# A two-layer graph network on one core: the order of work in layer 0's rounds, and where the first maxima of the attention are searched

## The chip, the core and the metric

The kernel runs on one core of a Trainium2 chip. A core has TensorE (PE, matrix products), VectorE (DVE), ScalarE (ACT), GpSimd (POOL) and SyncE (SP), which here issues every DMA. The metric is the device time in microseconds (us) of one execution; lower is better.

## What is computed

There are N = 3327 nodes with 128 features, and a dense 0/1 adjacency matrix with ones on its diagonal. Two layers follow each other, each with a residual sum and a layer norm:

```python
# layer 0: attention by cosine over the neighbours
norm2 = norm(x, axis=1)
cos   = beta * (x @ x.T) / (norm2 @ norm2.T + 1e-7)
P     = softmax(cos + (1 - adj) * -1e9, axis=1)
x     = layernorm(x + P @ x)
# layer 1: 128 heads of width 8, all over the whole graph
q, k, v = (x @ W.T).reshape(128, n, 8)  for W in (Wq, Wk, Wv)
a   = softmax(einsum('dnh,dmh->dnm', q, k) * 128**-0.5 + adj + adj, axis=2)
out = einsum('dnm,dmh->dnh', a, v).reshape(n, 1024) @ Wo.T
x   = layernorm(x + out)
```

## The kernel before

All is in float32; q and k of layer 1 are split into a high and a low part. The nodes are padded to T = 26 tiles of 128. The program has four stages.

**Layer 0** runs in rounds. In round t four tiles of rows are in hand at once, at different steps, and a list written out by hand (the loop over k from 0 to 7) says in which order each engine takes them up. PE, ACT, DVE and POOL each work through their own list strictly in that order. The steps, with the lines of the profile:

- `load` (L120): a tile's 128 rows of the adjacency, 1.66 MB, into one of three buffers `raw`; SP issues it.
- `adj_chunk` 0 to 6 (L166, L215): PE turns four 128x128 blocks of `raw` into a PSUM bank `tp`, ACT copies them into `aT`; with the seventh, SP writes the turned tile to memory for layer 1. There are two banks `tp`, shared with the turns of the weights.
- `mask` (L221): one POOL pass over `raw`, in place; it waits until PE has turned the last chunk.
- `inverse_log`, `inverse_exp` (L228, L231): two long ACT passes that give 1/(product of norms) as `y`. `inverse_product`, `inverse_newton` (L236, L242): two long DVE passes that refine `y`; the first makes `n` from `norm_k` and `y`, the second `y` from `n` and `y`.
- `scores` 0 to 3 (L190, L250, L253): PE multiplies a quarter of the columns, DVE combines it with `y` and then adds the mask and keeps a running minimum.
- `weights` (L269): two ACT passes, the exponential. `turn_weights` 0 to 6 (L166, then a copy to `pt`): PE turns four blocks of the weights, and DVE (even chunks, L156) or ACT (odd chunks, L154) copies them. `weigh0` (L288): PE multiplies the copied chunk with the features. There are two buffers `pt`.
- `norm_begin`, `norm_root`, `norm_end` (L295 to L322): the layer norm, in small steps on DVE, ACT and DVE. `project_turn`, `project` 0 to 5 (L330 to L347): the rows of q, k and v, by PE through one PSUM bank, ACT, and a write by SP.

**Splitting q and k** (L453 to L491): for each of 8 groups of 16 heads, a strided read of k, of q and of v (`nat`), a POOL pass that reorders it (L458), and for k and q seven turns on PE, the rounded high part by ACT (L469), the rest by DVE (L470), a POOL copy of the last column (L473), and two writes of 1.66 MB. Here the order is found by the scheduler, not by hand.

**Attention**: 288 units, each three tiles of queries by four heads, with 26 steps of 128 keys. A softmax needs the greatest score of a row first: the maxima are searched `T + AHEAD` = 33 steps ahead of the main loop, each step a pair (PE L616, DVE L631 or L642) and a single (L616, L652 or L656). So before the main loop starts, 33 steps run alone, after the loads of the first two units (L563 to L575) and beside the loads of the first adjacency block (L540, 26 of 96 KB). Then 26 ACT passes make `eT` from them (L547), and the first exponentials of the main loop (L840) stand behind these on ACT.

**The end** turns and projects the rows and does the last layer norm.

Of the kernel before, what the change touches and what calls it, by code (L numbers as in the profile page):

```python
# [10 lines left out]
F32 = mybir.dt.float32  # L11
F32R = mybir.dt.float32r
BF16 = mybir.dt.bfloat16
# [3 lines left out]
PSUM = bass.MemoryType.PSUM  # L17
# [29 lines left out]
def gnn_two_layers(  # L47
# [104 lines left out]
    def copy(i: int, dst: bass.AP, src: bass.AP):  # L152
        if i % 2:
            nc.scalar.copy(dst, src)  # L154
        else:
            nc.vector.tensor_copy(dst, src)  # L156
# [18 lines left out]
    with ExitStack() as l0:  # L175
# [23 lines left out]
        def load(t: int):  # L199
            u = tiles[t]  # L200
            u.raw = load_adj(adj_raw, t)
            u.xr = ptp.tile([P, D], F32, name="xr", bufs=5)
            if t < T - 1:
                nc.sync.dma_start(u.xr, node_rows(x, t, D))
            else:
                nc.gpsimd.memset(u.xr, 0.0)
                nc.sync.dma_start(u.xr[: P - 1], node_rows(x, t, D, P - 1))
# [66 lines left out]
        def turn_weights(t: int, c: int):  # L274
            u = tiles[t]
            if c == 0:
                u.pts = {}
            tp, a, b = turn(ps_tp, lambda k: u.s[:, k * P : (k + 1) * P], c)
            u.pts[c] = ptp.tile([P, 4, P], F32, name="pt")[:, : b - a, :], a, b
            copy(c, u.pts[c][0], tp)  # L280

        def weigh0(t: int, c: int):
            u = tiles[t]
# [22 lines left out]
        def norm_root(t: int):  # L306

            u = tiles[t]
            u.r = small.tile([P, 1], F32, name="r0")
            nc.scalar.activation(u.r, u.var, AF.Ln)  # L310
            nc.scalar.activation(u.r, u.r, AF.Exp, scale=-0.5)
# [37 lines left out]
        with tc.manual_schedule(  # L349
# [53 lines left out]
                nc.scalar.activation(piece(norm_k, j), score_piece(ones, sqT, j), AF.Sqrt)  # L403
            nc.scalar.preload_act_table_set("natural_log_exp_and_others")

            for t in range(-1, T + 2):

                def there(n: int):
                    return 0 <= n < T

                for k in range(8):
                    if k == 0 and there(t + 2) and t > 0:
                        load(t + 2)
                    if k == 0 and there(t - 2):
                        norm_begin(t - 2)
                    if k == 0 and there(t - 1):
                        weights(t - 1, 0)
                        weights(t - 1, 1)
                    if k == 1 and there(t - 2):
                        norm_root(t - 2)  # L420
                    if there(t) and k in (0, 2, 4, 6):
                        scores(t, k // 2)
                    if k == 2 and there(t - 2):
                        norm_end(t - 2)
                    if k < NCH and there(t + 1):
                        adj_chunk(t + 1, k)
                    if k == 1 and there(t + 1):
                        inverse_log(t + 1)
                    if k == 2 and there(t + 1):
                        inverse_exp(t + 1)  # L430
                    if k > 0 and there(t - 1):
                        turn_weights(t - 1, k - 1)
                        if k > 1:
                            weigh0(t - 1, k - 2)
                    if k == 3 and there(t - 2):
                        project_turn(t - 2)
                    if there(t - 2):
                        for i in {4: (0,), 5: (1, 2), 6: (3,), 7: (4, 5)}.get(k, ()):
                            project(t - 2, i)
                    if k == 6 and there(t + 1):  # L440
                        mask(t + 1)
                    if k == 7 and there(t + 1):
                        inverse_product(t + 1)
                        inverse_newton(t + 1)
                if there(t - 1):
                    weigh0(t - 1, NCH - 1)


    with ExitStack() as pr:
        work = pr.enter_context(tc.tile_pool(name="pr_work", bufs=2))  # L450
        ps_tp = pr.enter_context(tc.tile_pool(name="pr_tp", bufs=4, space=PSUM))

        for g in range(NG):  # L453
            for src, dst in ((k_s, kp_s), (q_s, qp_s)):
                nat = work.tile([P, HG, T * H], F32, name="nat")
                nc.sync.dma_start(nat, heads(src)[g])
                by_t = work.tile([P, T, P], F32, name="by_t")
                nc.gpsimd.tensor_copy(  # L458
                    by_t.rearrange("p t (g h) -> p g t h", h=H),
                    nat.rearrange("p g (t h) -> p g t h", h=H),  # L460
                )

                high = work.tile([P, NP], F32R, name="high")
                low = work.tile([P, NP], F32R, name="low")
                for c in range(NCH):
                    tp, a, b = turn(ps_tp, lambda t: by_t[:, t], c)
                    cols = slice(a * P, b * P)
                    tp = tp.rearrange("p t k -> p (t k)")
                    nc.scalar.copy(high[:, cols], tp)  # L469
                    nc.vector.tensor_sub(low[:, cols], tp, high[:, cols].bitcast(F32))  # L470

                for i, part in enumerate((high, low)):
                    nc.gpsimd.tensor_copy(  # L473
                        part[:, NP - 1 : NP], part[:, NP - 1 - P : NP - P].bitcast(F32)
                    )
                    nc.sync.dma_start(
                        dst[g * HG : (g + 1) * HG, :, i].rearrange("d f n -> (d f) n"),
                        part.bitcast(F32),
                    )
            nat = work.tile([P, HG, T * H], F32, name="nat")  # L480
            nc.sync.dma_start(nat, heads(v_s)[g])
            vals = work.tile([P, HG, T, H + 1], F32, name="vals")
            nc.gpsimd.memset(vals[:, :, :, H : H + 1], 1.0)
            nc.gpsimd.tensor_copy(
                vals[:, :, :, :H], nat.rearrange("p g (t h) -> p g t h", h=H)
            )
            nc.vector.tensor_scalar_mul(vals[:, :, T - 1], vals[:, :, T - 1], real)
            nc.sync.dma_start(
                vt_s[4 * g : 4 * g + 4].rearrange("a p h t f -> p a (h t f)"),
                vals.rearrange("p (a h) t f -> p a (h t f)", a=4),  # L490
            )  # L491

# [3 lines left out]


    with ExitStack() as at:  # L500
        fix = at.enter_context(tc.tile_pool(name="at_fix", bufs=1))
        keys = at.enter_context(tc.tile_pool(name="at_k", bufs=3))
        pp = at.enter_context(tc.tile_pool(name="at_p", bufs=4))
        sm = at.enter_context(tc.tile_pool(name="at_sm", bufs=2))
        ps_a = at.enter_context(tc.tile_pool(name="at_a", bufs=2, space=PSUM))
        ps_b = at.enter_context(tc.tile_pool(name="at_b", bufs=1, space=PSUM))
        ps_m = at.enter_context(tc.tile_pool(name="at_m", bufs=1, space=PSUM))
        ps_o = at.enter_context(tc.tile_pool(name="at_o", bufs=1, space=PSUM))

        QB = QT * P  # L510
        AHEAD, LAG = 7, 2
        acc = ps_o.tile([P, 512], F32, name="acc")
        nc.vector.memset(acc, 0.0)
        one = fix.tile([P, P], BF16, name="one")
        nc.vector.tensor_copy(one, ones)
        unit = fix.tile([P, P], BF16, name="unit")
        nc.vector.tensor_copy(unit, ident)

        nine = fix.tile([P, 4, H + 1], F32, name="nine")
        nc.vector.tensor_copy(  # L520
            nine, ident.rearrange("p (h x) -> p h x", h=4)[:, :, : H + 1]
        )

        parts = []
        for i in range(2):
            three = fix.tile([P, QT, 4, 32], BF16, name=f"parts{i}")
            nc.vector.memset(three, 0.0)
            parts.append(three)
        aT = fix.tile([P, T, QB], BF16, name="aT1")
        eT = fix.tile([P, T, QB], F32, name="eT1")  # L530

        units = [(b, g) for b in range(NB) for g in range(G4)]
        NU = len(units)
# [246 lines left out]
        with tc.manual_schedule(  # L780
# [4 lines left out]
                mybir.EngineType.Pool,  # L785
            }
        ):
            us = {0: load_unit(0), 1: load_unit(1)}
            steps = {}

            def max_step(k):
# [5 lines left out]
                    steps[i] = max_steps(2 * i, 2 * i + 1)  # L797
                return steps[i][j]

            def new_a():  # L800
                return [ps_a.tile([P, 512], F32, name="ea") for _ in range(2)]

            for j in range(T):
                load_adj_tile(0, j)
            for k in range(T + AHEAD):
                pair, single = max_step(k)
                max_pair(*pair)
                max_single(*single)
                if k == T:
                    shift_parts(us[0])  # L810
            e = ps_b.tile([P, 2, 512], F32, name="eb")
            for q in range(QT):
                shift_turn(us[0], q, e[:, 0, q * P : (q + 1) * P], True)
# [155 lines left out]
```

## Time and profile before

| | |
|---|---|
| time, median of 3 runs | 16088.82 us (16087.31 to 16089.61) |
| the profiled execution | 16094.0 us, of which its span 16092.2 us |
| layer 0, up to the last row write | to 955.7 us of the span |
| one round of layer 0 (combine of score piece 0 to the next) | 34.15 us |
| splitting q and k | 955.9 to 1253.4 us |
| first maxima alone | 1262.3 to 1331.5 us |
| first exponential of the main loop | 1343.2 us |
| main loop to its end | to 15975 us |

Times of instructions are counted from the first instruction of the span. In an answer by windows the columns are the stretch, then for PE, its weight loads, DVE, ACT and POOL the busy microseconds with the number of instructions, then the granted TensorE clock (1.00 is full speed), the share of the DMA engines' time that was used, and GB/s. A line of the timeline has the start, the length, the engine, the code line, the operation, output and input, and in brackets how long the engine stood idle and who ended that. Matmuls overlap, so the time that one takes from its engine is the distance to the next start.

### The profile page before, as it was taken

Reading aid. Unit: us, or ns where it says so; the run is one execution under the profiler, and the core shown is the slowest. Engines: PE = TensorE matmul, PEld = TensorE weight load, DVE = VectorE, ACT = ScalarE, POOL = GpSimd, SP = SyncE. Lnnn points to the kernel's source line nnn. Section 1 sums busy time; section 2 is a strip of 40 time slices with the busy share of each in tenths; the row PEclk is TensorE's granted clock in tenths of the full one; section 3 lists DMA queues with packets and bytes.
Section 4 is the critical chain, followed back from the end, with each engine's and each line's share of the span. In section 5 each row is a group of like instructions: output and inputs, shape, how many; then the busy total and the mean of one; then the engine's idle time right before and its main releaser. Section 6 shows DMA issues by size and latency. Waiting matters only on the chain.

```text
span 16092.2 us, 507025 instructions
## 1 busy us (share of the span) xinstructions
PE 15517.9 (96%) x217532; PEld 6935.5 (43%) x217532; DVE 13906.8 (86%) x16159; ACT 12637.3 (79%) x24904; POOL 13664.8 (85%) x9062
## 2 busy tenths in 40 slices
PE   6748999999999999999999999999999999999999
PEld 5533444444444444444444444444444444444555
DVE  6637999999999999999999999999999999998775
ACT  5525888888888888888888888888888888888776
POOL 1016999999999999999999999999999999998886
PEclk9978999999999999999999999999999999999999
DMA  3372111111111111111111111111111111111112
GB/s 128 126 269 94 47 50 50 51 50 50 48 53 50 50 44 57 50 47 48 57 50 45 50 52 51 48 50 50 51 50 50 47 54 50 50 45 60 61 61 75
DMA packets 483008, 995.72 MB, mean 62 GB/s; under 512 B 280274, under 2 KB 377424, under 8 KB 436208
## 3 DMA queue, kind: packets, MB, share of 16 engines
q1 hardware_dynamic: 480752, 963.28, 17.6%
q8 instruction: 1704, 27.92, 0.7%
q14 instruction: 552, 4.52, 0.1%
HBM read 813.16 MB, written 149.94 MB: 60 GB/s over the span
## 4 chain that ended last, share of the span: by engine, by line
PE 92%; DVE 4%; ACT 2%; DMA 1%; issue 1%; POOL 0%; SPq 0%; DVEq 0%; POOLq 0%; ACTq 0%
PE acc L725 28%; PE ea L695 20%; PE m L616 15%; PE eb L708 12%; PE ea L708 9%; PE ea L714 2%; PE eb L714 2%; DVE mx L631 1%; PE ea L681 1%; PE tp L166 1%; PE ea L743 1%; PE acc L288 1%; DVE y L242 1%; DVE n L236 1%; PE pq L342 1%
## 5 line engine op out<-in xcount | busy, mean ns | idle before, releaser
L841 POOL TENSOR_TENSOR pb<-pb,eT 128x768 f32<-128x768 f32 (+1 forms) x7488 | 13181.4, 1765 | 1103.4 <-ACT pb L840 858.6
L631 DVE TENSOR_REDUCE mx<-m 128x2 f32<-128x1024 f32 x6784 | 8274.2, 1220 | 516.8 <-PE eb L714 249.7
L840 ACT ACTIVATE pb<-eb 128x768 f32<-128x768 f32 (+1 forms) x7488 | 5896.9, 788 | 2507.8 <-PE eb L714 1772.7
L616 PE MATMUL m<-kx,qx 32*128 32x512 f32 (+1 forms) x23296 | 6781.8, 471 | 70.8 <-DVE mx L631 38.2
L870 ACT ACTIVATE pa<-ea 128x384 f32<-128x384 f32 (+1 forms) x14976 | 6339.7, 478 | 59.0 <-PE ea L695 45.2
L725 PE MATMUL acc<-pa,vt 128*9 128x384 f32 (+1 forms) x29952 | 5901.7, 474 | 0.0
L725 PE MATMUL acc<-pb,vt 128*9 128x384 f32 (+1 forms) x29952 | 5900.0, 474 | 0.1
L652 DVE TENSOR_REDUCE mx<-m 128x1 f32<-128x512 f32 x6400 | 4380.8, 685 | 691.1 <-PE m L616 317.9
L708 PEld LDWEIGHTS <-one 3*128 3x128 bf16 x29952 | 1507.8, 91 | 5564.2 <-issue 4665.8
L695 PE MATMUL ea<-aT,two 128*32 128x384 bf16 (+1 forms) x59904 | 3714.5, 325 | 0.0
L714 PE MATMUL ea<-qx,kx 32*128 32x384 f32 (+1 forms) x14976 | 3447.5, 437 | 0.0
L714 PE MATMUL eb<-qx,kx 32*128 32x384 f32 (+1 forms) x14976 | 3435.3, 451 | 0.0
L708 PE MATMUL ea<-cx,one 3*128 3x384 bf16 (+1 forms) x14976 | 3293.8, 322 | 2.9 <-ACT pa L870 0.2
L616 PEld LDWEIGHTS m<-kx,qx 32*128 32x128 f32 x23296 | 2815.0, 182 | 443.8 <-DVE mx L631 96.0
L708 PE MATMUL eb<-cx,one 3*128 3x384 bf16 (+1 forms) x14976 | 2461.6, 326 | 9.5 <-ACT pb L840 8.9
L725 PEld LDWEIGHTS acc<-pa,vt 128*9 128x9 f32 x29952 | 1413.2, 91 | 786.5 <-issue 0.7
L695 PEld LDWEIGHTS <-two 128*32 128x32 bf16 x59904 | 944.8, 94 | 1418.4 <-issue 1278.4
L714 PEld LDWEIGHTS eb<-qx,kx 32*128 32x128 f32 x14976 | 1460.7, 189 | 0.0
L714 PEld LDWEIGHTS ea<-qx,kx 32*128 32x128 f32 x14976 | 1431.8, 182 | 8.2 <-issue 4.1
L725 PEld LDWEIGHTS acc<-pb,vt 128*9 128x9 f32 x29952 | 1409.3, 91 | 0.6 <-POOL pb L841 0.6
L656 DVE TENSOR_REDUCE mx<-m 128x2 f32<-128x512 f32 x1088 | 748.3, 688 | 96.7 <-PE eb L714 44.1
L221 POOL TENSOR_SCALAR raw<-raw 128x3328 f32<-128x3328 f32 x26 | 78.6, 3022 | 738.7 <-PE tp L166 727.9
(124 smaller groups left out, 4976.6 us busy)
## 6 DMA issues: line engine op xcount, KB each, us to landing
kx<-kp_s SPq DMA_DIRECT2D x576, 832.0 KB, 4.8
vt<-vt_s SPq DMA_DIRECT2D x288, 468.0 KB, 4.9
qx<-qp_s SPq DMA_DIRECT2D x1024, 48.0 KB, 5.1
raw<-in_adj_dram SPq DMA_DIRECT2D x25, 1663.5 KB, 7.7
aT_s<-aT SPq DMA_DIRECT2D x26, 832.0 KB, 3.4
aT<-aT_s SPq DMA_DIRECT2D x208, 96.0 KB, 2.1
vt_s<-vals SPq DMA_DIRECT2D x8, 1872.0 KB
q_s<-row SPq DMA_DIRECT2D x26, 512.0 KB, 2.6
```

Of the source, the lines that this page charges most:

```text
L166: nc.tensor.transpose(tp[:, i, :], block(4 * c + i), ident)
L616: nc.tensor.matmul(dst, u.qx[rows(a), q * P : (q + 1) * P], u.kx[rows(a), k0:k1], start=True, stop=True,)
L631: nc.vector.tensor_reduce(u.mx[:, h, qs[0], c], m, axis=AX.X, op=ALU.max)
L652: nc.vector.tensor_reduce(u.mx[:, a, qs[0], c : c + 1], m, axis=AX.X, op=ALU.max)
L656: nc.vector.tensor_reduce(u.mx[:, a, qs[0] : qs[1] + 1, c], m.rearrange("p (q k) -> p q k", q=2), axis=AX.X, op=ALU.max,)
L695: nc.tensor.matmul(e[r, : u.nq], two[:, r], aT[:, j, : u.nq], start=False, stop=True, tile_position=(0, 32 * c), skip_group_check=True,)
L708: nc.tensor.matmul(e[:, : u.nq], one[r], u.cx[r, : u.nq], start=True, stop=False, skip_group_check=True)
L714: nc.tensor.matmul(e[:, : u.nq], u.kx[rows(a), j * P : (j + 1) * P], u.qx[rows(a), : u.nq], start=False, stop=stop, skip_group_check=True,)
L725: nc.tensor.matmul(acc[32 * h : 32 * h + H + 1, : u.nq], u.vt[:, h, j], pts[h // 2][:, h % 2, : u.nq], start=(j == 0), stop=(j == T - 1), ...
L840: nc.scalar.activation(pt_b[:, :, : u.nq], e_b[:, :, : u.nq], AF.Exp)
L841: nc.gpsimd.tensor_tensor(pt_b[:, :, : u.nq], pt_b[:, :, : u.nq], eT[:, j, : u.nq].unsqueeze(1).to_broadcast([P, 2, u.nq]), ALU.mult,)
L870: nc.scalar.activation(pt_a[:, h, : u.nq], e[:, : u.nq], AF.Exp)
```

## The change

In layer 0, ACT's long passes of a round come first: the exponentials of tile t-1, the root of tile t-2's norm, and the two passes that make `y` of tile t+1. Score pieces 0 and 1 are done together at the start, then 2 and 3. The adjacency is turned and masked two tiles ahead instead of one, in the second half of the round, and loaded three tiles ahead; there is one round more, at the start. All copies of turned weights go to DVE. The two refining passes come at k = 6, ahead of the last turned chunk, and the mask at k = 7.

The stage that splits q and k is now written out by hand inside the attention's schedule. Units 0 and 1 are loaded after the first group, and three steps of the first maxima follow each of the k and q splits from group 2 on. The last column is copied by DVE instead of POOL, and `vals` has one buffer instead of two. The pools for `aT1`, `eT1` and the main loop are opened only after that stage, so the loads of the first adjacency block come after it.

```diff
@@ turn_weights
-            copy(c, u.pts[c][0], tp)
+            nc.vector.tensor_copy(u.pts[c][0], tp)
@@ rounds of layer 0
-            for t in range(-1, T + 2):
+            for t in range(-2, T + 2):
...
                 for k in range(8):
-                    if k == 0 and there(t + 2) and t > 0:
-                        load(t + 2)
                     if k == 0 and there(t - 2):
                         norm_begin(t - 2)
                     if k == 0 and there(t - 1):
                         weights(t - 1, 0)
                         weights(t - 1, 1)
+                    if k == 0 and there(t - 2):
+                        norm_root(t - 2)
+                    if there(t):
+                        for i in {0: (0, 1), 2: (2,), 4: (3,)}.get(k, ()):
+                            scores(t, i)
+                    if k == 0 and there(t + 1):
+                        inverse_log(t + 1)
+                        inverse_exp(t + 1)
                     if k == 1 and there(t - 2):
-                        norm_root(t - 2)
-                    if there(t) and k in (0, 2, 4, 6):
-                        scores(t, k // 2)
-                    if k == 2 and there(t - 2):
                         norm_end(t - 2)
-                    if k < NCH and there(t + 1):
-                        adj_chunk(t + 1, k)
-                    if k == 1 and there(t + 1):
-                        inverse_log(t + 1)
-                    if k == 2 and there(t + 1):
-                        inverse_exp(t + 1)
                     if k > 0 and there(t - 1):
                         turn_weights(t - 1, k - 1)
                         if k > 1:
                             weigh0(t - 1, k - 2)
                     if k == 3 and there(t - 2):
                         project_turn(t - 2)
+                    if there(t + 2):
+                        for i in {3: (0, 1), 4: (2,), 5: (3, 4), 6: (5,), 7: (6,)}.get(k, ()):
+                            adj_chunk(t + 2, i)
+                    if k == 5 and there(t + 3) and t >= 0:
+                        load(t + 3)
                     if there(t - 2):
                         for i in {4: (0,), 5: (1, 2), 6: (3,), 7: (4, 5)}.get(k, ()):
                             project(t - 2, i)
                     if k == 6 and there(t + 1):
-                        mask(t + 1)
-                    if k == 7 and there(t + 1):
                         inverse_product(t + 1)
                         inverse_newton(t + 1)
+                    if k == 7 and there(t + 2):
+                        mask(t + 2)
                 if there(t - 1):
                     weigh0(t - 1, NCH - 1)
@@ splitting q and k, now within the attention's hand-written schedule
-            us = {0: load_unit(0), 1: load_unit(1)}
+            us = {}
...
-            for j in range(T):
-                load_adj_tile(0, j)
-            for k in range(T + AHEAD):
+            def first_max(k):
                 pair, single = max_step(k)
                 max_pair(*pair)
                 max_single(*single)
                 if k == T:
                     shift_parts(us[0])
...
+                def prepare(g, src, dst):
...
+                    for i, part in enumerate((high, low)):
+                        nc.vector.tensor_copy(
+                            part[:, NP - 1 : NP], part[:, NP - 1 - P : NP - P].bitcast(F32)
+                        )
...
+                k = 0
+                for g in range(NG):
+                    for src, dst in ((k_s, kp_s), (q_s, qp_s)):
+                        prepare(g, src, dst)
+                        for _ in range(3 if g > 1 else 0):
+                            if k < T + AHEAD:
+                                first_max(k)
+                                k += 1
+                    prepare_values(g)
+                    if g == 0:
+                        us[0], us[1] = load_unit(0), load_unit(1)
+                while k < T + AHEAD:
+                    first_max(k)
+                    k += 1
+
+            fix = at.enter_context(tc.tile_pool(name="at_fix", bufs=1))
...
+            aT = fix.tile([P, T, QB], BF16, name="aT1")
+            eT = fix.tile([P, T, QB], F32, name="eT1")
+            for j in range(T):
+                load_adj_tile(0, j)
```

## The prediction

> **What bounds the kernel now.** I read the busy time by stage first, here layer 0 from its first combine, the split of q and k, the first maxima, and the main loop.
>
> ```profile
> 63.00:956.00 893.00, 676.70 (x3408) 513.25 (x3408) 564.36 (x753) 463.61 (x638) 77.87 (x51) 0.93 0.32 117
> 956.00:1253.00 297.00, 81.23 (x416) 73.59 (x416) 70.32 (x120) 58.94 (x112) 81.39 (x63) 0.60 1.03 375
> 1253.00:1333.00 80.00, 46.02 (x126) 20.42 (x126) 61.14 (x72) 0.93 (x3) 0.94 (x4) 0.50 0.41 122
> 1333.00:15975.00 14642.00, 14610.17 (x212849) 6238.69 (x212848) 13153.07 (x15068) 12075.19 (x24100) 13485.58 (x8923) 1.00 0.15 51
> ```
>
> The main loop is PE's (14610 of 14642) and its list is not changed: I take 0 for it. The split is the DMA engines' (share 1.03, no compute engine over 82 of 297). The maxima are DVE's (61 of 80). Layer 0 belongs to nobody: PE 676 of 893, DVE 564. So I read the chain of waits there; one round looks like this:
>
> ```profile
> 301.16 2.99 DVE s L253
> 304.49 3.60 DVE n L236
> 308.12 3.62 DVE y L242
> 314.14 2.97 ACT y L228
> 317.58 2.88 ACT y L231
> ```
>
> DVE's refining passes, then ACT's two passes with PE's copies behind them, 34.15 us a round. The minimum at 301.16 takes 2.99 where its sisters take 1.08: POOL's mask runs from 300.31 for 2.97. The start of the program shows what that pair does to the refining passes (timelines of DVE, then POOL):
>
> ```profile
> 52.91 3.69 DVE L236 SCALAR_TENSOR_TENSOR n<-norm_k,norm_c,y 128x3328 f32<-128x3328 f32 x1 [14.82 <-ACT y L231]
> 56.63 6.26 DVE L242 SCALAR_TENSOR_TENSOR y<-n,y 128x3328 f32<-128x3328 f32 x1
> ```
> ```profile
> 55.12 4.30 POOL L221 TENSOR_SCALAR raw<-raw 128x3328 f32<-128x3328 f32 x1 [14.31 <-PE tp L166]
> ```
>
> The mask is released during the first pass, waits for its end, and then runs before the second pass: 1.3 + 2.97 = 4.30, and the second pass takes 6.26 instead of 3.62. Last, PE's clock, in stretches as long as the clock's own steps (3.41 us):
>
> ```profile
> 317.50:320.92 3.42, 0.78 (x5) 0.53 (x4) 1.47 (x7) 3.42 (x4) 0.00 (x0) 1.00 0.06 19
> 320.92:324.33 3.41, 3.34 (x14) 3.17 (x15) 0.69 (x1) 0.77 (x3) 0.00 (x0) 0.50 0.00 0
> 1037.70:1041.10 3.40, 1.63 (x10) 1.04 (x10) 3.01 (x6) 1.45 (x3) 0.00 (x0) 1.00 1.03 410
> 1167.40:1170.80 3.40, 1.57 (x13) 1.21 (x11) 3.24 (x7) 2.20 (x5) 1.84 (x2) 1.00 1.11 347
> ```
>
> A stretch in which PE is busy 0.78 of 3.41 is followed by one at half clock, in every round. The same befell 1.63 at 1037.7, but not 1.57 at 1167.4, nor 1.74 at 95.6. The edge lies at some 1.6.
>
> **A round, walked through.** PE's prices are distances between starts:
>
> ```profile
> 326.37 1.06 PE L288 MATMUL acc<-xn,pt 128*128 128x128 f32 x8
> 327.26 1.02 PE L342 MATMUL pq<-wq,x1T 128*128 128x512 f32 x2
> 328.12 0.62 PE L166 MATMUL tp<-ident,raw 128*128 128x128 f32 x4
> 328.57 0.60 PE L166 MATMUL tp<-ident,s 128*128 128x128 f32 x4
> 329.01 1.06 PE L288 MATMUL acc<-xn,pt 128*128 128x128 f32 x8
> ```
>
> A weighing costs 0.89, a projection 0.86, a group of four turns 0.44; a score piece 1.4 (1.56 until DVE may read). On DVE a score piece takes 2.12, the norm's end 1.1, a copy 0.65. Zero is DVE's first combine. Scores 0 and 1 to 4.2, norm end to 5.3, copy 0 done at 6.0; score piece 2 to 8.0, copy 1 done at 8.7. Weighing 1 waits for that. From 8.7 PE has work in hand: weighings 1 to 3 (2.7), the turn of x1 (0.2), chunks 0 to 4 (2.2), scores 3 (1.4), turns 3 and 4 (0.9), projections 0 to 2 (2.6) and once the wait for the one bank (0.9, as at 331.62): 10.9, so turn 5 starts at 19.6. Its copy lets DVE begin the first refining pass at 20.9, to 24.6.
>
> Now the mask: it needs the last chunk, and PE gets there 0.44 + 0.89 + 0.44 + 0.86 + 0.22 + 0.89 + 0.38 = 4.1 after turn 5 starts, at 23.7: 0.9 before the first pass ends. That is the case of 55.12, so the second pass ends 6.3 later, at 30.9, not 3.6 later, at 28.3. Queued behind it on DVE stands the copy of chunk 6 (0.41), for which PE's weighing 6 waits, and behind that in PE's list scores 0 of the next round: 30.9 + 0.4 + 0.5 + 1.6 = 33.4 for the next combine. Before, at full clock, the round is 34.15 less what the half-clock stretch costs: 320.99 to 325.48 is 4.49 for work worth 0.44 + 0.89 + 0.2 + 1.4 = 2.93, thus 32.6. ACT's saving (the three copies, 1.75, and the wait of 2.63 behind its long passes) is spent: DVE takes the copies (+2.0), and what is late next is DVE's second pass.
>
> The clock: PE ends its last projection near 26.9 and waits over 4 us for weighing 6. A stretch of 3.41 with nearly nothing in it follows, so weighing 6 and scores 0 and 1 run at half clock: +1.9 on the way to the combine, +0.4 for piece 1: 35.7. A second place is the wait for copies 0 and 1: the 3.41 us before weighing 1 hold weighing 0 and a group of turns, 1.5 busy with their ends. That is below 1.63 and 1.57, so I take the half clock for the next stretch too; it costs 1.6 as before: **37.3**. Layer 0: 26 x (37.3 - 34.15) = **+82**. If the second stretch keeps its clock: 26 x 1.55 = +40.
>
> The Trainium skill (TensorE: Matmul & The Clock Gate, HAM oscillation) asks only that PE have no gap over some 3.4 us. In this trace the longest gap of a round, 2.63, already loses the clock, so the measurement decides; by the page alone the round would be 35.7.
>
> The rest of the rounds, edits with one answer: the load of tile t+3 goes out when score piece 3 frees its buffer, near 15, and is needed near 10 of the next round, over 25 us later against 7.7 to land: 0, and if SP held it so long, 26 times what is late. On SP it moves behind x1's write and ahead of the rows of q: 0.3 us of issue. The extra first round does work that is dropped later: 0.
>
> **The split and the maxima.** The 33 steps cost 2.12 each (1263.18, 1265.30), 70 us. In the new place they are 3 steps or 6.4 us of DVE per split, beside 37 us of DMA per group, in which DVE is busy 9: hidden; without that cover they cost up to 70. Against that:
> - Units 0 and 1 are now read while the DMA engines are full: 4.65 MB at 375 GB/s, 12. On SP these reads stand behind the first group's value write and ahead of the second group's key writes, and wait until the first group has landed (up to 17.1, as the value write issued at 1025.57); the engines are moving those writes meanwhile, so 0, with 10 as the upper end.
> - The first adjacency block waits until the split's buffers are free, that is for its last write:
>
> ```profile
> 1238.10 15.24 DMA vt_s<-vals
> 1257.15 5.21 DMA vt<-vt_s
> ```
> ```profile
> 1263.49 15.98 SPq L540 DMA_DIRECT2D aT<-aT_s  x26
> ```
>
> So 1253.4 + 12 = 1265.4; 26 issues 16.0; landing 2.1; the last exponential 0.5 (the others, 0.42 each, keep up with issues of 0.61): the main loop's first exponential at 1284 instead of 1343.2. Before, these loads lay under the maxima. Gain **-59**, with ends -45 (the 10 above and slower issues) and -65.
> - The copies of the last column on DVE: the rival below. One buffer of `vals`: a write is long landed when the next group's values come, 37 us later: 0.
>
> Sum on the profiled execution: 16094.0 + 82 - 59 = 16117. The median lies 5.2 below that execution: **16112**.
>
> **Rivals.**
> 1. *The clock falls once a round.* 1.57 busy kept it at 1167.4. Then 40 - 59 = -19: 16070. Chance 0.24.
> 2. *The mask comes too late to step between the passes.* If PE's list is 0.9 us later there, POOL takes its turn after the second pass and hits nothing. The round is 33.4 - 2.6 = 30.8 at full clock, with one or two half-clock stretches 32.4 to 34.1: -45 to 0, with the split -104 to -59, middle 16007. Against it: 4.1 us of list without a wait on another engine. Chance 0.12.
> 3. *Slower: the last-column copies, now from SBUF to SBUF on DVE, wait for POOL's reordering pass* (2.96 each), as the minimum waits for the mask. No row shows such a copy beside a POOL pass; bounds 0 and 16 x 2.96 = 47. It decides only where the write behind it comes after the DMA engines have run dry, that is where DMA's share falls below 1; today over 10 us of transfers wait in line mostly. I take 0. With 47: 16159. Chance 0.07.
>
> In the Trainium skill, SBUF — State Buffer (Who interferes with whom) lets a plain copy block that way, which speaks for rival 3 as a mechanism; no run here shows it for these copies.
>
> **How the numbers follow.** My forecast has 0.55, the others 0.24, 0.12 and 0.07, with 0.02 for what I do not see. The forecast's own spread is 15 us each way (14 between the ends of the split, a tenth of a microsecond or two per round): 16097 to 16128. About 0.2% (32 us, to 16121) is what a measurement of this kernel can tell from no change; a third of the forecast lies above it. Slower: 0.2 + 0.07 + 0.01 = 0.28. Faster (below 16057): 0.12 + a tenth of rival 1 and a little = 0.15. Same: 0.57. The range takes in rival 1 and the upper half of rival 2, and the spread upward with a third clock stretch: 16035 to 16145.
>
> **What would show it.** Right: rounds of 36 to 37.5 us; L242 at 6.2 with L221 starting during L236; two or three half-clock stretches a round; the maxima inside the split; first exponential of the main loop 50 to 60 us sooner after the split's start. Wrong: L242 at 3.6 in the rounds; rounds below 34; DMA's share in the split below 0.95, or a main loop that is not 14642 long.

## The result, and the profile after

The changed kernel takes 16068.7 us (median of 20 runs, 16065.2 to 16072.1), the kernel before 16086.8 us (20 runs, 16084.5 to 16089.6): a ratio of 0.9989, 95% interval 0.9982 to 0.9996. It is 18 us or 0.11% faster, less than the 0.2% that the prediction gives as what one measurement of this kernel can tell from no change. I had forecast 16112, 23 us above the old median. The sign was wrong, and by the parts below the error lies almost wholly in one term: the price of the half clock.

The busy time by stage after (layer 0 from its first combine, the split with the maxima in it, the loads of the first adjacency block, the main loop):

```profile
63.00:1007.50 944.50, 702.51 (x3401) 501.44 (x3400) 627.82 (x833) 432.08 (x556) 93.32 (x49) 0.87 0.29 111
1007.50:1316.00 308.50, 114.85 (x523) 89.70 (x523) 134.15 (x220) 58.77 (x112) 78.43 (x36) 0.61 1.01 376
1316.00:1333.50 17.50, 2.80 (x31) 1.65 (x32) 2.28 (x5) 12.30 (x28) 0.00 (x0) 0.50 0.78 186
1333.50:15950.00 14616.50, 14594.03 (x212806) 6251.14 (x212805) 13145.69 (x15066) 12061.30 (x24073) 13488.60 (x8922) 1.00 0.16 51
```

Layer 0 is longer (944.5 instead of 893), and its clock is granted at 0.87 instead of 0.93. The split is 11.5 longer and still full of DMA (share 1.01); DVE's busy time in it went from 70 to 134, the maxima that no longer stand by themselves. From its first to its last wide exponential the main loop takes 14617 instead of 14631, 14 less, which I had put at 0. (Its window before, 14642 long, begins 10 us ahead of the first exponential.)

The chain of waits in one round after:

```profile
501.64 6.26 DVE y L242
508.31 1.20 PE acc L288 x4
509.51 2.70 PE sc L190 x4
512.24 1.09 DVE s L250
```

The second refining pass, weighing 6, scores 0, the next combine: the way that the prediction walked. And POOL's mask in the next round (timeline of POOL, then of DVE):

```profile
537.00 3.51 POOL L221 TENSOR_SCALAR raw<-raw 128x3328 f32<-128x3328 f32 x1 [9.27 <-PE tp L166]
```
```profile
537.72 6.26 DVE L242 SCALAR_TENSOR_TENSOR y<-n,y 128x3328 f32<-128x3328 f32 x1
```

The mask is released 0.7 before the first pass ends (0.9 forecast), waits for that end, and the second pass waits for the mask: 6.26, in every full round. But the rounds come in pairs of 36.17 and 35.51, a mean of 35.84, and not the 37.3 of the forecast. In each round the clock falls to a half for two steps at weighing 6 and scores 0 (6.83 us); in every other round it falls once more, for one step, after the wait for copy 0. PE's clock over such a pair, in windows on the clock's own steps, with the weighing 0 that ends the wait (timeline of PE):

```profile
515.38:518.80 3.42, 1.11 (x9) 0.87 (x8) 3.24 (x10) 1.70 (x1) 0.00 (x0) 1.00 0.06 19
518.80:522.21 3.41, 3.17 (x15) 2.77 (x15) 2.72 (x5) 0.00 (x0) 0.00 (x0) 0.50 0.00 0
552.93:556.35 3.42, 1.59 (x12) 1.36 (x12) 3.28 (x7) 0.23 (x1) 0.00 (x0) 1.00 0.06 19
556.35:559.76 3.41, 2.57 (x19) 2.52 (x20) 1.38 (x4) 1.06 (x3) 0.00 (x0) 1.00 0.00 0
```
```profile
518.29 1.63 PE L288 MATMUL acc<-xn,pt 128*128 128x128 f32 x8 [2.31 <-DVE pt L280]
554.47 1.16 PE L288 MATMUL acc<-xn,pt 128*128 128x128 f32 x8 [1.68 <-DVE pt L280]
```

In one round the wait is 2.31 long and lies whole in one step, which is left with 1.11 of work; the next step runs at half clock. In the other round scores 0 and 1 ran at half clock for longer (5.02 instead of 4.29), so PE comes later to the same wait. It is 1.68 long, its step holds 1.59 of work, and the clock stays.

Behind layer 0, from the chain of waits:

```profile
1301.58 14.38 DMA vt_s<-vals
1329.66 2.96 DMA aT<-aT_s
```

The split's last write lands, 26 issues of 0.53 each follow (0.61 before), and the main loop's first exponential comes at 1333.5: 325.9 after the split's start, where it was 387.3.

### The profile page after: what moved, and what is told of

The parts are those of the page before. It is cut to its first block, busy times and chain, and to the rows that moved or that the text cites. A ratio compares the mean times of both kernels' runs of the same rounds, so it can differ in the third digit from the quotient of the medians.

```text
span 16067.9 us, 507030 instructions
## 1 busy us (share of the span) xinstructions
PE 15521.0 (97%) x217532; PEld 6936.2 (43%) x217532; DVE 13964.9 (87%) x16269; ACT 12606.0 (78%) x24826; POOL 13681.2 (85%) x9030
## 4 chain that ended last, share of the span: by engine, by line
PE 92%; DVE 5%; DMA 1%; ACT 0%; issue 0%; POOL 0%; SPq 0%; DVEq 0%; POOLq 0%; ACTq 0%
PE acc L663 28%; PE ea L633 20%; PE m L554 15%; PE eb L646 12%; PE ea L646 9%; PE eb L652 2%; PE ea L652 2%; DVE mx L569 1%; PE ea L619 1%; DVE y L242 1%; PE tp L166 1%; PE acc L288 1%; PE sc L190 1%; PE ea L681 1%; DVE mx L590 1%; DVE n L236 1%
## 5 line engine op out<-in xcount | busy, mean ns | idle before, releaser
L652 PE MATMUL eb<-qx,kx 32*128 32x384 f32 (+1 forms) x14976 | 3473.2, 454 | 0.0
```

The lines of the kernel that those rows point to most:

```text
L652: nc.tensor.matmul(e[:, : u.nq], u.kx[rows(a), j * P : (j + 1) * P], u.qx[rows(a), : u.nq], start=False, stop=stop, skip_group_check=True,)
```

## The experiments

Kernels that ran together share their runs of the kernel before: its median was 16086.2 beside the first four, 16092.1 beside the next four and 16092.0 beside the last. So each result is given as the difference to that as well. The changed kernel itself stands at -18.1, and "below the changed kernel" is counted from there. The theory at the start: the round goes through both refining passes, made long by the mask, and then through weighing 6 and scores 0, with a price for each half-clock stretch on top. Its rivals: the mask has nothing to do with it; the passes alone hold the round; the price of the clock is something else.

**e1 and e2, each half of the change alone.** e1 has the new layer 0 before the old split, e2 the old layer 0 before the new split.

```diff
 e1, layer 0 alone: the first part of the change
-            copy(c, u.pts[c][0], tp)
+            nc.vector.tensor_copy(u.pts[c][0], tp)
-            for t in range(-1, T + 2):
+            for t in range(-2, T + 2):
...
 e2, behind layer 0 alone: the second part
-            us = {0: load_unit(0), 1: load_unit(1)}
+            us = {}
...
+                        for _ in range(3 if g > 1 else 0):
```

> The new rounds and the copies on DVE alone; everything behind layer 0 as before the change. Theory (the parts of the change add up, and the main loop does not depend on layer 0): layer 0 ends 51.7 us later than before, as in the changed kernel (1007.6 against 955.9), so 16087 + 52 = 16139, and the main loop lasts 14631 from its first to its last exponential, as in the profile of before. Rival (the 14 us by which the main loop of the changed kernel is shorter come with the rounds, or differ from one execution to the next): 16125 to 16133, or a main loop that is neither 14631 nor 14617.

> The split of q and k with the maxima in it alone, layer 0 as before the change. From the start of the split to the first exponential of the main loop 326 us as in the changed kernel, instead of 387: -61. Theory (the shorter main loop comes with this part, which opens the main loop's tiles later and so in other places): main loop 14617, total 16087 - 61 - 8 to 14 = 16012 to 16018. Rival (the main loop's length is a spread between executions): total 16026, and a main loop of 14631 or something else again.

e1: 16130.2, **+44.0** (ratio 1.0028, 1.0017 to 1.0038). e2: 16025.1, **-61.1** (0.9962, 0.9950 to 0.9975). Their sum, -17.1, is the -18.1 of the whole change: the parts add up. The main loop from first to last of its 7488 wide exponentials took 14631 in the profile of before, 14619 in e1, 14621 in e2, and 14617 to 14624 in all the other profiles here. e1 runs the old code there, so no part of the change shortened it: the one profiled execution of before was long. The rivals got both totals (16125 to 16133, and 16026); my theory on the main loop fell. Layer 0 ends 46.4 later in e1's profile, not the 51.7 expected: the changed kernel's profile has one early round of 38.05 where e1's takes 35.59.

**e3, the mask away from the passes.**

```diff
-                u.aT = ptp.tile([P, T, P], BF16, name="aT", bufs=1)
+                u.aT = ptp.tile([P, T, P], BF16, name="aT", bufs=2)
...
+                    if k == 2 and there(t + 1):
+                        adj_chunk(t + 1, 6)
+                        mask(t + 1)
                     if there(t + 2):
-                        for i in {3: (0, 1), 4: (2,), 5: (3, 4), 6: (5,), 7: (6,)}.get(k, ()):
+                        for i in {3: (0, 1), 4: (2,), 5: (3, 4), 6: (5,)}.get(k, ()):
                             adj_chunk(t + 2, i)
...
-                    if k == 7 and there(t + 2):
-                        mask(t + 2)
```

> The changed kernel, with the last turned chunk and the mask of a tile taken one round later, at k = 2 (and a second buffer for the turned tile), so that the mask is not released during the first refining pass. Theory (the second pass is long because the mask steps between the two): L242 takes 3.62 instead of 6.26 in every round, the copy of chunk 6 ends 2.6 us sooner, the round goes from 35.84 to 33.2: 16069 - 26 x 2.6 = 16000; if one of the half-clock stretches goes too, down to 15960. Rival 1 (L242 is long for another reason, its place behind the first pass for one): L242 stays at 6.26 and the total within 10 us of 16069. Rival 2 (the mask costs the same wherever it runs, since DVE then waits elsewhere): L242 3.62, but a minimum (L253) or copies (L280) longer by up to 3 us, total above 16040.

16007.2, -79.0 (0.9951, 0.9938 to 0.9963), and 61 below the changed kernel (69 expected). In the timelines of DVE and POOL:

```profile
533.37 3.62 DVE L242 SCALAR_TENSOR_TENSOR y<-n,y 128x3328 f32<-128x3328 f32 x1
```
```profile
549.52 2.98 POOL L221 TENSOR_SCALAR raw<-raw 128x3328 f32<-128x3328 f32 x1 [26.13 <-PE tp L166]
```

L242 is back at 3.62 in every round, the mean round is 33.03 (33.2 expected). Both rivals fall: the pass was long because of the mask, and where the mask now lies, beside DVE's copies out of PSUM, those are no longer than elsewhere (0.69 each, at 549.15 and 551.05).

**e4, chunk 6 copied ahead of the passes.**

```diff
-                        turn_weights(t - 1, k - 1)
+                        if k < 7:
+                            turn_weights(t - 1, k - 1)
                         if k > 1:
                             weigh0(t - 1, k - 2)
+                        if k == 6:
+                            turn_weights(t - 1, 6)
```

> The changed kernel, with the turn and the copy of chunk 6 ahead of the two refining passes, so that PE's weighing 6 and the next scores 0 wait for neither pass. Theory (the round goes through the second pass, the copy of chunk 6 behind it, weighing 6 and scores 0, partly at half clock): the passes start 1.0 us later (turn 6 goes ahead of it), L242 still takes 6.26 and ends 1 us later, but the next combine follows its end by only the 1.4 us of the norm's begin, where it now follows by 4.5: the round is shorter by 2.0 to 2.2, some 33.7, total 16069 - 26 x 2.1 = 16014, and no half-clock stretch at weighing 6. Rival (the passes themselves set the round, and PE's work behind them is hidden or comes at the same time): the round is longer by the 1.0 that the passes are put off, total 16095.

16026.4, -59.8 (0.9963, 0.9951 to 0.9976): 42 below the changed kernel where 55 was expected, rounds of 34.13 (33.7 expected). The combine does follow the norm's begin directly. What I missed is where PE's wait goes. Its next score pieces need the banks that the combines free (timeline of PE):

```profile
516.13 3.07 PE L190 MATMUL sc<-xT 128*128 128x416 f32 x8
523.60 3.15 PE L190 MATMUL sc<-xT 128*128 128x416 f32 x4 [3.96 <-DVE s L250]
```

so it stands 4 us later in the round instead, and score piece 2, which takes 1.67 at full clock, takes 3.15. Weighing 6 and scores 0 were on the path, as the theory had it.

**e5 and e7, the passes earlier.** DVE stood idle for 3.2 to 3.75 and for 4.3 us in each round, while the passes waited behind its copies. e5 puts each pass into one of these gaps; e7 gives the odd copies back to ACT and changes nothing else.

```diff
 e5
+                    if k == 3 and there(t + 1):
+                        inverse_product(t + 1)
+                    if k == 5 and there(t + 1):
+                        inverse_newton(t + 1)
...
-                    if k == 6 and there(t + 1):
-                        inverse_product(t + 1)
-                        inverse_newton(t + 1)
 e7
-            nc.vector.tensor_copy(u.pts[c][0], tp)
+            copy(c, u.pts[c][0], tp)
```

> The changed kernel, with the first refining pass put behind DVE's copy of chunk 2 and the second behind its copy of chunk 4, where DVE stands idle 3.75 and 4.3 us. Theory (the round is as long as the way through both passes, with PE's weighing 6 and scores 0 behind them): both passes (3.68 and 3.62) lie in idle time, L242 is no longer beside the mask, PE goes from its last projection straight to weighing 6 and scores 0: the next combine at about 541.2 after 512.2 in the profile of the changed kernel, a round of 29.0 to 29.5, total 16069 - 26 x 6.5 = 15900. Rival (the passes now hold up score piece 3 and the copies of chunks 3 to 5, and PE behind them): rounds of 32 and more, total above 15970.

> The changed kernel, with the copies of the odd chunks of turned weights on ACT again, as before the change. Theory (in the changed kernel the first refining pass stands behind DVE's copy of chunk 5, 4.3 us later than it could start; with that copy on ACT it stands behind the copy of chunk 4): L236 starts 4.9 us earlier against the round, both passes are over before the mask is released, L242 takes 3.62, and PE's weighing 6 no longer waits: rounds of 29 to 30, total 16069 - 26 x 6.3 = 15905. Rival (the copies on ACT are as late as before the change, behind its long passes, and PE waits for them): rounds of 32 to 34, total 15970 to 16020.

e5: 15930.4, -161.7 (0.9901, 0.9887 to 0.9914), rounds between 29.1 and 31.3, 30.13 in the mean. That is 144 below the changed kernel where 169 was expected; the rounds above 31 are those with two half-clock steps, the others have one or none. e7: 15912.3, -179.7 (0.9889, 0.9875 to 0.9902), 162 below the changed kernel (164 expected), rounds of 28.69 and 29.33. In e7 (timelines of DVE, POOL and PE):

```profile
530.75 3.63 DVE L242 SCALAR_TENSOR_TENSOR y<-n,y 128x3328 f32<-128x3328 f32 x1
```
```profile
534.94 2.96 POOL L221 TENSOR_SCALAR raw<-raw 128x3328 f32<-128x3328 f32 x1 [9.16 <-PE tp L166]
```
```profile
537.36 0.61 PE L288 MATMUL acc<-xn,pt 128*128 128x128 f32 x4
```

The second pass ends at 534.4, before the mask is released; PE goes to weighing 6 with no wait. Undoing this one edit gains more than three times the 44 that the new rounds lose: moving the three odd copies to DVE is what costs. With it the first pass stands behind the copy of chunk 5, and the rest follows. The other edits of the rounds were not undone one by one.

**e6 and e8, the price of the clock.** PE gets work that changes no value in its two waits (e6), or in the first alone (e8).

```diff
 e6 and e8, in turn_weights
+            if c == 1:
+                for _ in range(4):
+                    ... the four transposes of chunk 1 again, into the same tp
 e6 alone, in project
+            for _ in range(5 if k == 5 else 1):
                 nc.tensor.matmul(pq, u.x1T, ws[n][:, cols], start=True, stop=True)
```

> The changed kernel, with work for PE in its two waits: the four turns of chunk 1 done five times instead of once (1.8 us more, in the wait for the copies 0 and 1), and the last projection done five times (3.4 us more, in the wait for weighing 6). Theory (the half clock is what the round costs above 33.4, and it is set by how much of a clock step PE is busy): no half-clock stretch is left, scores 0 and 1 take 1.4 and 1.5 instead of up to 4.3 together, the round is 33.4, total 16069 - 26 x 2.44 = 16005. Rival (the clock falls for another reason, or the stretches cost nothing since DVE's passes set the round): rounds of 35.8 or more, total 16069 or above.

> The changed kernel, with only the first of the two fillings: the four turns of chunk 1 done five times, in PE's wait for the copies 0 and 1. Theory (the third half-clock stretch, which comes in every other round, is this wait falling into one step of the clock's fixed grid): two stretches a round are left, rounds all alike at 35.2 to 35.5, total 16069 - 26 x 0.3 to 0.6 = 16053 to 16061. Rival (a half-clock stretch here costs the 1.6 us that the prediction gave it): 35.84 - 0.8 = 35.04, total 16048 or less; second rival (it costs nothing): 16069.

e6: 16043.4, -48.7 (0.9969, 0.9957 to 0.9982). e8: 16066.4, -25.7 (0.9985, 0.9976 to 0.9993). A round of e6 by windows, and its weighing 6 in PE's timeline:

```profile
498.00:531.83 33.83, 29.41 (x157) 21.56 (x157) 24.53 (x34) 17.10 (x22) 3.61 (x2) 1.00 0.33 126
```
```profile
520.87 0.71 PE L293 MATMUL acc<-xn,pt 128*128 128x128 f32 x4 [1.35 <-DVE rden L300]
```

No stretch at half clock is left, the mask still steps between the passes (L242 6.26), and the round is 33.83 throughout. So the clock costs 35.84 - 33.83 = 2.01 a round. In e8 the stretch after the wait for copy 0 is gone, and from one stretch at weighing 6 to the next the clock is whole (the window lies 0.3 us behind the clock's steps, hence 0.99):

```profile
509.79:537.10 27.31, 22.71 (x139) 17.26 (x137) 19.26 (x24) 12.15 (x17) 3.61 (x2) 0.99 0.37 144
```

The mean round of e8 is 35.66: the stretch that comes in every other round is worth 0.18, the one in every round 1.83. The rounds of e8 are not all alike at 35.2 to 35.5, as I had expected; they run from 35.1 to 36.0, so 0.18 is a difference of means. Both totals missed. e8 is 7.5 below the changed kernel, just short of the 8 to 16 expected. e6 is 31 below instead of 64. Its round is 33.83 and not 33.4, its fillings also run in the last two rounds, which have no waits to fill (80.3 from the last tile's first combine to the split, instead of 70.4), and one late round took 38.25; some 8 of the difference are left open.

**e9, what holds e7.** In e7, PE at full clock waits 2.3 and 1.1 us a round for copies 0 and 1 behind DVE's score pieces. e9 puts both copies on DVE, between the score pieces: scores 0, turn 0 and its copy, scores 1, turn 1 and its copy, the norm's end, scores 2.

```diff
-            nc.vector.tensor_copy(u.pts[c][0], tp)
+            copy(0 if c == 1 else c, u.pts[c][0], tp)
...
```

> The kernel with the odd copies on ACT (e7), with the copies of chunks 0 and 1 both on DVE and put between the score pieces (after piece 0 and after piece 1), and the norm's end behind them. Theory (with the passes out of the way the round is PE's list plus its waits for the copies 0 and 1, 2.3 and 1.1 us, behind DVE's pieces and the norm's end): the turn of x1 comes 6.7 us after the first combine instead of 9.8; ACT's long passes end 8.2 after it and hold the copy of x1 for up to 1.5 of that, so the round is shorter by 1.9 to 3.1, 25.9 to 27.1, total 15912 - 26 x 1.9 to 3.1 = 15832 to 15863. Rival (the round is held by PE's list with its waits for the one bank of the projections, or by ACT): rounds above 28, total 15890 or more.

15872.5, **-219.5** (0.9863, 0.9847 to 0.9880), rounds of 27.40, above the 25.9 to 27.1 expected; it is 40 below e7 where 49 to 80 was expected. What comes last now, in PE's timeline:

```profile
528.18 0.72 PE L166 MATMUL tp<-ident,raw 128*128 128x128 f32 x4 [1.51 <-ACT aT L215]
```

PE waits twice 1.5 us for banks that ACT, still in its long passes, has not emptied. This is the fastest version run here, 1.4% below the kernel before.

## Why the prediction was wrong, step by step

- **The way of a round: right.** The mask released during the first pass, the second pass at 6.26, weighing 6 and scores 0 behind it: all as walked, and e3, e4 and e7 each take one link away and gain. The round at full clock was put at 33.4 and is 33.83 in e6.
- **The clock: the step that failed, "it costs 1.6 as before: 37.3".** Forecast +2.3 and +1.6 a round, measured +1.83 and +0.18 (e6, e8). Over 26 rounds that makes 26 x (37.3 - 35.84) = 38 us, of the 43 by which the total missed. Two things were wrong with the second stretch. I weighed "the 3.41 us before weighing 1", as if a step always ended there. The steps lie on a fixed grid: in one round of a pair a step ends at 518.80, 2.2 ahead of weighing 1, and holds 1.11; in the other a step holds just the work that I weighed (1.59; I had put 1.5), and the clock stays. And I carried its price over from a row of before in which PE then had an unbroken row of work. Here PE waits for copy 1 inside the slow stretch (timeline of PE, the slow and the fast round):

```profile
521.01 1.72 PE L288 MATMUL acc<-xn,pt 128*128 128x128 f32 x8 [0.24 <-DVE pt L280]
557.19 1.16 PE L288 MATMUL acc<-xn,pt 128*128 128x128 f32 x8 [1.13 <-DVE pt L280]
```

  Both start 8.8 us after their round's first combine. The slow weighing 0 and turn before it only shorten the wait, from 1.13 to 0.24; what is lost is the longer weighing 1, some 0.55. In every other round that is 0.28 a round; e8 gave 0.18. e7 shows the grid best: PE's wait for copy 0 is 2.3 long in both rounds of a pair (2.31 before 516.24, 2.32 before 545.58), and the clock falls only behind the first, which lies whole in a step; an edge, at 544.2, cuts the second. The edge of the busy time itself, some 1.6, was right: steps with up to 1.13 busy were followed by half clock in the changed kernel, steps with 1.59 and more were not.
- **Layer 0 as a whole:** +82 forecast, +44 by e1. In the changed kernel's profile it ends 51.7 later: 43 of that are rounds, 8 lie behind the first combine of the last tile (in e1's profile 46.4: 41 and 5). I had counted 26 rounds and no such rest.
- **Split and maxima: right.** -59 forecast, -61.1 by e2. The unit loads moved the last write by 11 (12 forecast), the issues of the first adjacency block took less than before. Rival 3 cost nothing: all 16 copies of a high part took the same time (shortest, median and longest in ns), and so did those of a low part:

```profile
L769 DVE CAST high<-high x16: 153/153/154, 1025.8 to 1300.5; 128x1 fp32r<-128x1 f32 x16
```

  Only one of these 16, at 1030.01, begins beside a POOL pass (1027.16, 2.98 long), so what the pair does to each other is hardly tried by this.
- **The main loop: 0 was right.** That its window came out at 14617 instead of 14642 was one of my marks for "wrong". It marked nothing of the change: 11 us of it are where the window of before begins and ends, and the other 14 are the one profile of before, as e1 shows. The forecast was right to take off the 5.2 by which that execution lies above its median; the median of 20 runs is 2 lower still.
- **Rival 1 had the number** (16070, at 0.24), not quite the mechanism: the clock does fall a second time, in every other round, and then costs little.
- The Trainium skill (TensorE: Matmul & The Clock Gate, HAM oscillation) asks for no gap over some 3.4 us, which gave 35.7. That is close to the 35.84, by chance in part: in this trace a wait of 2.31 already loses the clock. The same page (Part 1: The HAM clock gate) says that the window is free-running. The grid here bears that out, as it runs on through all rounds in steps of 3.41, and I had not used it.

## What to carry to other kernels

When an operation is taken off one engine's list, look at what now stands behind it on the other: three copies of 0.65 us cost nearly 7 us a round (28.98 in e7 against 35.84), because a long pass came to stand behind a copy that waits for PE. A price for a slow clock is walked on the path like any other, since a wait inside the slow stretch hides it; and whether a stretch falls is read on the clock's own grid, not from the instruction of interest. A stage that the change does not touch, and that still differs between two profiles, calls for a third profile before it is explained. A wait can also hide another one: what fills or shortens it lets the hidden one out (the late round, below).

## What the runs showed of the hardware

- Changes of the clock lie on a grid: every stretch in layer 0 here is a multiple of 3.41 us. So is the pair of rounds after (71.68 = 21 x 3.413), the pair of e7 (58.02 = 17 x 3.413), and the round of before and of e4 (34.13 = 10 x 3.413). Whether the rounds fall into step with the grid because of the stretches was not tried apart; in the two kernels whose steady rounds have no stretch the round is no multiple (e6: 33.83; e9: 27.40 beside 27.31).
- The edge, from 300 to 750 us of every kernel's trace: a full-clock step with less than 1.59 of 3.41 us busy was always followed by half clock, one with more than 1.71 never, and between them both occurred (1.59 kept the clock, 1.70 in e3 lost it). In the changed kernel a half-clock step with 1.75 busy was followed by another, one with 3.16 and more by full clock.
- The 16 transposes that filled e8's wait, where the changed kernel had one step in two rounds at half clock, kept it whole: they count as work for the clock.
- In all nine kernels with the new rounds, one write of q's rows, issued just behind the last tile's adjacency load, takes 4.6 to 5.7 to issue instead of 0.3; why was not tried. In the changed kernel it is issued at 854.10 (4.93) and lands 9.9 later. ACT's next piece of v's rows waits for that, and PE's last projection waits 4.62 instead of 0.69. In the changed kernel, e1, e4 and e8 the round in which this falls is at most 0.5 longer, and PE has a wait of some 4 us or more just behind it in every round, which can hide it. In e3, e5, e6, e7 and e9, where that wait is shorter, gone or filled, the round is 2 to 6 longer.
